# A decoder layer on one core: one product of v placed behind the third outer products, a later first turn in the drain, and small weights loaded ahead of the mixtures

## The chip, the core and the metric

The kernel runs on one core of one Trainium2 chip, in float32. The metric is the device time of one execution in microseconds (us). It is compared as the median of several executions; one further execution was taken by the profiler, and every row of a profile is from that one.

## The reference, cut to what matters

The layer has three parts, each added to x (32 sequences of 64 tokens, 512 wide, so 2048 tokens):

```python
x = x + attention(layernorm(x))       # 32 heads of 128; q and k get a bias and an rmsnorm with gains
x = x + cross_attention(layernorm(x), ctx)   # 64 x 64 weights Wq, Wk, Wv, Wskip
x = x + experts(layernorm(x))         # router 512 -> 64, top 8, mixture of expert biases
```

In the attention, `q = rmsnorm(xn @ Wq + bq) * gq`, the same for k, `v = xn @ Wv + bv`, and `out = softmax(q k^T / sqrt(128)) v @ Wo + bo`. The four projections (512 by 4096, and 4096 by 512) are nearly all of the arithmetic.

## The kernel before, in words

**Projections by Strassen's scheme.** A 2 by 2 block product is made with seven block products instead of eight. Tokens go in halves of the batch (two), a half in two quads of 512 tokens; heads go in 16 groups of two. For each half, the first head group takes its quads one by one (`single`, L1183). The other 15 take both quads together in a `Window` (L609, run by `double`, L1194): there q and k use the scheme twice over, an outer product that is itself made of seven inner ones. So there are 30 windows.

**A window's order of work is written by hand.** TensorE (PE in the profile), VectorE (DVE), ScalarE (ACT) and GpSimd (POOL) each run their instructions in program order. `Window.project` (L696) goes through four sets n = 0 to 3 of outer products: (1, 5), (2, 6), (7, 3) and (4). Each set is cut into four pieces m = 0 to 3 by the `yield`s of `outer` (L632). A piece issues p_w products on PE (L640) and DVE or ACT instructions that take their results out of PSUM (L651, L661, L664, L654). After each piece come, in this order: the entry of the table `behind` (L722), one waiting DVE step, and the entry of the table `plan` (L1201). I write (n, m) for such a place. The entries of `behind` that matter here are

```python
                (2, 2): lambda: (add(0, (1, 0), (1, 1)), add(0, (1, 1), (0, 1)), squares(1, 0, 0)),
                (2, 3): lambda: (add(1, (1, 0), (1, 1)), squares(1, 1, 0), squares(1, 0, 1)),
```

`add` with a first argument of 0 is a POOL addition, with 1 a DVE addition (both L719). `squares` is an ACT activation (L341) of the sum just made.

**v's products.** The plan also places v's seven products for each of the two quads (`values`, L363): one `v` in the plan is one product of 8 matmul instructions in the trace (L372). Their order is 1, 2, 6, 5, 7, 4, 3. Products 1, 6, 7 and 4 all add up in one PSUM tile, `va`, and after each of them ACT copies `va` to SBUF (L388), so that the next of them must wait for that copy. Products 2, 5 and 3 use the tile `vb`; DVE adds them to the copies (L392). In the kernel before, the first quad has its seven at (0,0) to (0,3) and (1,0) to (1,2), the second at (2,0) to (2,3) and (3,0) to (3,2).

**The rest of the attention** is pushed along by `Line` (L1137): `scale` multiplies q and k by their inverse norms (DVE L529, POOL L527, after a DMA of the norms), `attend` makes scores (L540), softmax (L254 to L262) and mixtures (L577), `turn` transposes the probabilities (L246).

**The drain.** After the last window, `drain` (L1321) makes the output projection of the first two token tiles (`plain_out`, 32 chunks of 8 matmul instructions, L822), and between chunks the line's remaining steps; `go(k)` runs k chunks. From chunk 24 on, DVE and POOL make the sums of Wo for Strassen's scheme (`wo_sums`, L858 to L866).

**The tails' start.** Then a new pool is opened. SyncE's queue (SP) issues nearly every DMA in program order, and so an issue that must wait holds up all that follow. In the kernel before it issues, in this order: bo_b; the mixtures a22, a11 and a21 of pair 1 (L806, 1 MB each); x for tile 3 (L173), whose buffer comes free when POOL has added bo to tile 1 (L810); eight small loads of the cross-attention's weights into `xw` (L214); rwt, rb_b and eb_sb. POOL fills `xw` with zeros first (L1372). PE makes five chunks of pair 1's output (product 2 of `strassen_out`, L869, on a mixture loaded earlier, is four of them; the fifth is the first of product 4, on a22), then two transposes of `xw` (L1392) and a product of them (L1396), and goes on with pair 1. Pairs 1 to 7 then run with the cross-attention and the experts of the tiles ahead (the tails) between their chunks.

Of the kernel before, what the change touches and what calls it, by code (L numbers as in the profile page):

```python
# [41 lines left out]
def decoder_layer(  # L42
# [37 lines left out]
    def block(name):  # L80
        return blocks.tile([P, BLK], F32, tag="blk", name=name)
# [130 lines left out]
    def load(to, what):  # L212

        tc.keep_in_program_order(nc.sync.dma_start(out=to, in_=what))  # L214
# [53 lines left out]
    def take_waiting():  # L268
        if waiting:
            waiting.pop(0)()  # L270
# [532 lines left out]
    def load_mixed(t, h, it):  # L803

        it = it.rearrange("p (g n) -> p g n", n=P)
        nc.sync.dma_start(out=it, in_=mixed[t // NQ][:, h, t % NQ, :, :])  # L806
        return it
# [41 lines left out]
    def wo_sums(b):  # L849

        four = four_blocks("wo_t")
        t1, t2 = (
            [it.rearrange("p (g f) -> p g f", f=DH) for it in two] for two in (four[0:2], four[2:4])
        )
        t4 = []
        for half in range(2):
            b11, b12, b21, b22 = (b[k][n][half] for k in range(2) for n in range(2))
            nc.vector.tensor_tensor(t1[half], b12, b11, ALU.subtract)  # L858
            nc.vector.tensor_tensor(t2[half], b22, t1[half], ALU.subtract)
            if half == 1:  # L860
                yield
            t4.append(block(f"wo_t4{half}").rearrange("p (g f) -> p g f", f=DH))
            nc.vector.tensor_tensor(t4[half], b21, t2[half], ALU.subtract)
        for half in range(2):
            b12, b22 = (b[k][1][half] for k in range(2))
            nc.gpsimd.tensor_tensor(b12, b22, b12, ALU.subtract)  # L866
        yield {1: b[0][0], 2: b[1][0], 3: b[1][1], 4: t4, 5: t1, 6: t2, 7: b[0][1]}
# [313 lines left out]
    line = Line()  # L1181
# [12 lines left out]
    def double(window, more):  # L1194

        v = window.v

        def end():
            line.attend(window.sums_of_squares, window.deviations)

        plan = [  # L1201
            [[v], [v], [v, line.scale], [v]],
            [[v, line.scale], [v, line.turn], [v], [line.attend, line.scale]],
            [[v, line.scale], [v], [v], [v]],
            [[v], [v], [v, line.turn], [*more.pop((3, -1), ()), end]],
        ]
        for (n, m), them in more.items():
            plan[n][m].extend(them)
        window.project(plan)
        line.add(*window.units)  # L1210
# [24 lines left out]
    for n, (hg, half) in enumerate(groups):  # L1235
# [29 lines left out]
        else:  # L1265
# [30 lines left out]
            if n + 1 == len(groups):  # L1296
                four = four_blocks("wo_0")
                wo_b = [[load_wo(k, 0, four[2 * k : 2 * k + 2])] for k in range(2)]
                a_0 = [[load_mixed(0, h, block(f"a0_{h}")) for h in range(HG)]]
            double(Window(units, w, half), more)  # L1300
    for k in range(2):
        wo_b[k].append(load_wo(k, 1, [block(f"wo{k}1{i}") for i in range(2)]))
# [18 lines left out]
    def drain():  # L1321
        fill = iter(todo)

        def go(count):
            for _ in range(count):
                next(fill)
                take_waiting()

        go(1)
        line.turn()  # L1330
        go(4)
        line.scale()
        go(4)
        line.scale()
        go(3)
        line.attend()
        line.scale()
        go(4)
        line.scale()
        go(1)  # L1340
        line.turn()
        go(2)
        line.attend()
        go(4)
        line.turn()
        go(1)
        line.attend()
        a12 = load_mixed(2, 1, block("a12_1"))
        sums = wo_sums(wo_b)
        next(sums)  # L1350
        for _ in fill:
            pass
        return a12, sums
# [4 lines left out]
    a_0.append([load_mixed(1, 0, block("a1_0")), load_mixed(1, 1, rest)])  # L1358
    todo = plain_out(0, a_0, wo_b, start_tail)
    a12, sums = drain()  # L1360
    assert not waiting and not coming
    ordered.close()
# [2 lines left out]
    bo_b = work.tile([P, D], F32, tag="bo", name="bo_b", bufs=1)  # L1365
    load(bo_b, bo.partition_broadcast(P))
    (right,) = sums
    outs = {1: strassen_out(1, right, start_tail, a12)}
    next(outs[1])

    xw = work.tile([P, 4, P], F32, tag="xw", name="xw", bufs=1)
    nc.gpsimd.memset(xw, 0.0)  # L1372
    for j, src in enumerate((xwq_t, xwk_t, xwv_t, xws_t)):
        for b in range(2):
            half = slice(b * SEQ, (b + 1) * SEQ)
            load(xw[half, j, half], src)
    rwt = work.tile([P, KC, NEXP], F32, tag="rwt", name="rwt", bufs=1)
    load(rwt, rw_t.rearrange("(kc p) e -> p kc e", p=P))
    rb_b = work.tile([P, NEXP], F32, tag="rb", name="rb_b", bufs=1)
# [4 lines left out]
    nc.gpsimd.memset(eb_sb[NEXP:P, :], 0.0)  # L1384
    nc.gpsimd.memset(wds, 0.0)
    load(eb_sb[0:NEXP, :], eb)
    for _ in range(4):
        next(outs[1])

    pt = ps_t.tile([P, 2, P], F32, tag="pt", name="pt_xw")  # L1390
# [64 lines left out]
```

## Time and profile before, and how to read it

| | |
|---|---|
| median of 3 executions | 1939.29 us (1936.71 to 1942.11) |
| the profiled execution | 1943.95 us |
| its span, first to last instruction | 1942.2 us, 1.75 us less |
| mean granted TensorE clock | 0.989 |
| PE busy | 1891.5 us, 97% of the span |
| DVE, POOL, ACT busy | 1211.4, 1046.5 and 643.6 us |
| one window, from one to the next at the same place | 42.34 us (603.60 to 645.93) |
| windows of the first half, of the second | from about 77 to 690 us, and from about 767 to 1391 us |
| drain | from 1393.4 us |
| tails' start | about 1464.5 us |

A row of a timeline gives the start in us from the span's beginning, the duration in us (of several merged instructions, from the first's start to the last's end), engine, source line, operation, output and inputs, the number of merged instructions, and in brackets the idle time of that engine before it with what ended it. PE's matmuls overlap a little: a row of four p_w instructions lasts 1.03 us, but the next row can start 0.86 us after it. Such distances from start to start are what a matmul costs when PE does not wait.

### The profile page before, as it was taken

To read this page: it belongs to the slowest core of one execution; us is meant where nothing else is said; L and a number is where in the kernel's file an instruction comes from. 1 tells how busy PE (TensorE), PEld (TensorE's weight loads), DVE (VectorE), ACT (ScalarE), POOL (GpSimd) and SP (SyncE) were. 2 spreads that over 40 slices of the span, in tenths; PEclk is the share of its full clock that TensorE was granted. 3 is DMA by queue.
4 is the path that set the end of the run, shared out by engine and by line. 5 is a ranking of instruction groups with operands and counts; after the bars stand their busy time and mean duration, and the time that the engine had idled before them with its cause. 6 is when DMAs were issued, how large, how long until landed. Compare 5 with 4: busy or idle time off the path is not lost.

```text
span 1942.2 us, 40532 instructions
## 1 busy us (share of the span) xinstructions
PE 1891.5 (97%) x16877; PEld 1628.0 (84%) x16877; DVE 1211.4 (62%) x2024; ACT 643.6 (33%) x1567; POOL 1046.5 (54%) x816
## 2 busy tenths in 40 slices
PE   8999999999999999999999999999998999999997
PEld 7888888888888878888888888888887888888875
DVE  5766767766667667766666666666545445554545
ACT  2244334344433443334433333443311112221122
POOL 4865667665567548666557666655225323332320
PEclk9999999999999999999999999999999999999998
DMA  4234333333433343333443333344933232223100
GB/s 132 66 99 129 123 111 109 110 99 117 131 125 100 109 141 101 101 107 99 127 133 113 110 109 100 99 130 135 300 118 128 90 106 70 69 90 112 49 20 22
DMA packets 162264, 210.72 MB, mean 108 GB/s; under 512 B 9888, under 2 KB 134880, under 8 KB 157984
## 3 DMA queue, kind: packets, MB, share of 16 engines
q1 hardware_dynamic: 160896, 207.05, 33.1%
q8 instruction: 133, 2.18, 0.5%
q10 hardware_dynamic: 1184, 1.08, 0.2%
q14 instruction: 51, 0.42, 0.1%
HBM read 169.82 MB, written 38.27 MB: 107 GB/s over the span
## 4 chain that ended last, share of the span: by engine, by line
PE 76%; DVE 11%; POOL 7%; issue 3%; DMA 2%; ACT 1%; SPq 0%; POOLq 0%; DVEq 0%; ACTq 0%
PE p_w L640 24%; PE py L822 18%; PE va L372 7%; PE vb L372 6%; POOL qk L719 5%; PE s L540 3%; PE ms_w L764 3%; PE o L577 3%; DVE qk L651 3%; DVE qk L664 3%; PE pa L430 1%; PE pt_p L246 1%; DVE qk L529 1%; DVE sums L259 1%; PE e_x L998 1%
## 5 line engine op out<-in xcount | busy, mean ns | idle before, releaser
L640 PE MATMUL p_w<-x,w 128*128 128x256 f32 x2940 | 726.0, 384 | 13.1 <-DVE qk L651 8.9
L640 PEld LDWEIGHTS p_w<-x,w 128*128 128x128 f32 x2940 | 522.3, 191 | 76.0 <-DVE qk L651 15.5
L651 DVE TENSOR_TENSOR qk<-p_w,qk 128x512 f32<-128x512 f32 x360 | 213.0, 599 | 148.6 <-PE p_w L640 113.0
L341 ACT ACTIVATE sq<-qk 128x512 f32<-128x512 f32 x256 | 158.2, 629 | 397.4 <-POOL qk L719 227.2
L372 PEld LDWEIGHTS va<-w,x 128*128 128x128 f32 x2048 | 265.3, 192 | 28.6 <-ACT v L388 18.3
L372 PE MATMUL va<-w,x 128*128 128x128 f32 x2048 | 277.2, 279 | 0.5 <-ACT v L388 0.5
L822 PE MATMUL py<-wo,a 128*128 128x256 f32 x1152 | 262.5, 381 | 0.0
L664 DVE TENSOR_TENSOR qk<-p_w,qk 128x512 f32<-128x512 f32 x360 | 219.7, 619 | 58.8 <-PE p_w L640 55.3
L120 POOL TENSOR_TENSOR w<-w 128x768 f32<-128x768 f32 x126 | 247.2, 1973 | 2.4
L822 PEld LDWEIGHTS py<-wo,a 128*128 128x128 f32 x1152 | 213.9, 190 | 35.6 <-issue 7.3
L262 POOL TENSOR_TENSOR prob<-prob,inv 128x512 f32<-128x512 f32 x64 | 76.7, 1198 | 293.5 <-DVE inv L261 292.5
L527 POOL TENSOR_TENSOR qk<-qk,rs 128x512 f32<-128x512 f32 x128 | 169.2, 1322 | 118.7 <-DMA rs<-row_w 98.6
L372 PEld LDWEIGHTS vb<-w,x 128*128 128x128 f32 x1536 | 202.3, 192 | 9.8
L372 PE MATMUL vb<-w,x 128*128 128x128 f32 x1536 | 203.3, 275 | 0.0
L388 ACT COPY v<-va 128x256 f32<-128x256 f32 x256 | 94.8, 370 | 320.5 <-PE va L372 320.4
L529 DVE SCALAR_TENSOR_TENSOR qk<-qk,gqk,rs 128x512 f32<-128x512 f32 x128 | 166.4, 1300 | 11.6 <-DMA rs<-row_w 10.2
L822 PE MATMUL py<-wo_t,a 128*128 128x256 f32 x608 | 142.2, 384 | 0.0
L822 PEld LDWEIGHTS py<-wo_t,a 128*128 128x128 f32 x608 | 114.6, 192 | 16.2 <-issue 0.8
L719 POOL TENSOR_TENSOR qk<-qk 128x512 f32<-128x512 f32 x60 | 90.3, 1504 | 60.6 <-DVE qk L664 58.2
L254 DVE TENSOR_REDUCE mx<-s 128x8 f32<-128x512 f32 x64 | 44.2, 691 | 110.0 <-PE s L540 110.0
L392 DVE TENSOR_TENSOR v<-vb,v 128x256 f32<-128x256 f32 x192 | 80.7, 420 | 47.9 <-PE vb L372 27.3
L592 ACT ACTIVATE ot<-o,bvt 128x256 f32<-128x256 f32 x256 | 99.2, 469 | 2.2 <-PE o L577 2.2
(177 smaller groups left out, 2191.4 us busy)
## 6 DMA issues: line engine op xcount, KB each, us to landing
rs<-row_w SPq DMA_DIRECT2D x120, 512.0 KB
mixed<-ot SPq DMA_DIRECT2D x64, 512.0 KB
a<-mixed SPq DMA_DIRECT2D x32, 1024.0 KB
w<-in_wq_dram SPq DMA_DIRECT2D x64, 256.0 KB
w<-in_wk_dram SPq DMA_DIRECT2D x62, 256.0 KB
w<-in_wv_dram SPq DMA_DIRECT2D x62, 256.0 KB
wo<-in_wo_dram SPq DMA_DIRECT2D x8, 1024.0 KB
x<-in_x_dram SPq DMA_DIRECT2D x28, 256.0 KB
```

Of the source, the lines that this page charges most:

```text
L120: on.tensor_tensor(*(it.rearrange("p c j d -> p (c j) d") for it in (out, a, b)), ALU.subtract)
L341: nc.scalar.activation(sq, of, AF.Square)
L372: nc.tensor.matmul(to[:, j, :], left[i][:, c, j, :], right[i][:, c, 2, :], start=first and j == 0 and c == 0, stop=c == 1, skip_group_chec ...
L388: nc.scalar.copy(self.v[h, ab], what)
L527: nc.gpsimd.tensor_tensor(k, k, rk, ALU.mult)
L529: lambda: nc.vector.scalar_tensor_tensor(q, q, gqk, rq, ALU.mult, ALU.mult)
L592: nc.scalar.activation(ot[:, h, :, b * SEQ : (b + 1) * SEQ], o[b][:, h, :, :], AF.Identity, bias=bvt[:, hg * HG + h : hg * HG + h + 1],)
L640: nc.tensor.matmul(bank[:, s, :], self.w.inner[o][i], inner_x[self.half, o][i], start=first and s == 0, stop=True, skip_group_check=True,)
L651: nc.vector.tensor_tensor(to(t, j), bank, add(t, j), ALU.add)
L664: nc.vector.tensor_tensor(to(t, j), bank, to(t, j), ALU.add)
L719: on.tensor_tensor(qk[to], qk[to], qk[what], ALU.add)
L822: nc.tensor.matmul(py, a[:, g, :], b[g // KH][:, g % KH, :], start=n == 0 and g == 0, stop=n == last and g == NHG - 1,)
```

## The change

Three edits. One `v` goes from place (0, 3) to place (2, 3), where there are now two, so that the first quad's last product of v (product 3) comes at (2, 0), and the second quad's seven at (2, 1), (2, 2), twice at (2, 3), and at (3, 0) to (3, 2). In the drain the first turn comes after three chunks rather than one, and the two scales behind it after six and nine chunks rather than five and nine. At the tails' start, the zeros and the eight loads of `xw` stand ahead of pair 1's mixtures in the program, and pair 1 gets six chunks rather than five ahead of the transposes of `xw`.

```diff
@@ double, L1201 @@
         plan = [
-            [[v], [v], [v, line.scale], [v]],
+            [[v], [v], [v, line.scale], []],
             [[v, line.scale], [v, line.turn], [v], [line.attend, line.scale]],
-            [[v, line.scale], [v], [v], [v]],
+            [[v, line.scale], [v], [v], [v, v]],
             [[v], [v], [v, line.turn], [*more.pop((3, -1), ()), end]],
         ]
@@ drain, L1329 @@
-        go(1)
+        go(3)
         line.turn()
-        go(4)
+        go(3)
         line.scale()
-        go(4)
+        go(3)
         line.scale()
@@ tails' start, L1365 @@
     (right,) = sums
-    outs = {1: strassen_out(1, right, start_tail, a12)}
-    next(outs[1])
 
     xw = work.tile([P, 4, P], F32, tag="xw", name="xw", bufs=1)
     nc.gpsimd.memset(xw, 0.0)
@@
             load(xw[half, j, half], src)
+    outs = {1: strassen_out(1, right, start_tail, a12)}
+    next(outs[1])
     rwt = work.tile([P, KC, NEXP], F32, tag="rwt", name="rwt", bufs=1)
@@
-    for _ in range(4):
+    for _ in range(5):
         next(outs[1])
```

## The prediction, made before the changed kernel had run

> **What bounds the kernel now.** First the page's busy times: PE is at work for 97% of the span, so only two things move the end, PE's work and PE's waits. The change adds no matmul and drops none.
>
> ```profile
> PE 1891.5 (97%) x16877; PEld 1628.0 (84%) x16877; DVE 1211.4 (62%) x2024; ACT 643.6 (33%) x1567; POOL 1046.5 (54%) x816
> ```
>
> Then the list of waits, for who keeps whom (total us, times, longest). ACT's squares (L341) wait for POOL's additions (L719) twice in each of the 30 windows, up to 9.5 us. ACT has time for that; the second line shows where it reaches PE, in the weight loads of v's products behind ACT's copies, 58 times, about two per window.
>
> ```profile
> ACT sq L341 <- POOL qk L719: 227.2, 60, 9.5
> PEld va L372 <- ACT v L388: 18.3, 58, 0.9
> ```
>
> Then the timeline of one window's end, all engines. It starts at place (2, 2).
>
> ```profile
> 640.93 1.05 PE L372 MATMUL va<-w,x 128*128 128x128 f32 x8
> 640.96 1.27 DVE L664 TENSOR_TENSOR qk<-p_w,qk 128x512 f32<-128x512 f32 x2
> ...
> 642.31 3.11 POOL L719 TENSOR_TENSOR qk<-qk 128x512 f32<-128x512 f32 x2 [2.16 <-DVE qk L664]
> 642.68 1.05 PE L372 MATMUL vb<-w,x 128*128 128x128 f32 x8
> ...
> 643.62 0.63 ACT L341 ACTIVATE sq<-qk 128x512 f32<-128x512 f32 x1 [6.47 <-POOL qk L719]
> 644.16 0.35 ACT L388 COPY v<-va 128x256 f32<-128x256 f32 x1
> 644.56 1.16 PE L372 MATMUL va<-w,x 128*128 128x128 f32 x8
> ...
> 645.45 1.15 ACT L341 ACTIVATE sq<-qk 128x512 f32<-128x512 f32 x2 [0.94 <-POOL qk L719]
> 645.46 0.42 DVE L651 TENSOR_TENSOR qk<-p_w,qk 128x256 f32<-128x256 f32 x1 [1.16 <-POOL qk L719]
> 645.93 1.13 PE L640 MATMUL p_w<-x,w 128*128 128x256 f32 x4 [0.21 <-DVE qk L651]
> ...
> 646.51 0.35 ACT L388 COPY v<-va 128x256 f32<-128x256 f32 x1
> 646.91 1.16 PE L372 MATMUL va<-w,x 128*128 128x128 f32 x8
> ```
>
> To be seen: DVE ends (2, 2) at 642.23, POOL makes two additions until 645.42, and three things hang on the second: a DVE step at 645.46 that holds PE (0.21 us), and ACT's two squares. PE's product of v at 646.91 starts 0.05 us after ACT's copy ended at 646.86. Last, the same view at the tails' start:
>
> ```profile
> 1463.03 0.53 POOL L1372 MEMSET xw<- 128x512 f32 x1
> ...
> 1464.52 1.89 PE L822 MATMUL py<-wo_t,a 128*128 128x256 f32 x8
> ...
> 1467.56 1.20 SPq L214 DMA_DIRECT2D xw<-in_xwq_t_dram  x2
> ...
> 1470.42 0.45 PE L1392 MATMUL pt_xw<-ident,xw 128*128 128x128 f32 x1 [4.01 <-POOL x L810]
> ```
>
> PE waits 4.01 us for loads issued behind the x of tile 3.
>
> **What the Trainium skill says.** "Perfetto Trace Analysis", section "Tensor Engine Instruction (MATMUL, LD_WEIGHTS)": ACT, DVE and GpSimd are strict FIFO. The trace agrees: PE had ended v's product 6 at 641.98, but its copy ran at 644.16, behind a square queued ahead of it. "GPSIMD Engine Reference", section "1. Specifications": its SBUF interfaces are shared with VectorE, with contention when a DVE instruction has two SBUF inputs. The trace agrees: L529, with two such inputs, took 0.70 us at 637.33 and 2.35 at 620.59, beside two of POOL's L120. "TensorE: Matmul & The Clock Gate", section "What's actually happening": an idle window of about 3.4 us halves the clock, a busy one restores it. The trace agrees: PE idle from 1466.41, granted clock 0.50 from about 1470 until 1476.8, and 24 matmuls from 1473.01 took 7.04 us, where they take 5.19 at full clock: 1.85 us lost.
>
> **Edit 1, v's product: what it removes.** The v product moved is 5, eight matmuls without a copy of its own; its addition on DVE goes with product 7's. At (2, 3) PE gets 0.89 us more work (eight v matmuls, start to start). The wait before (3, 1) goes: the v row ahead takes 1.37 us rather than 0.89 (644.56 to 645.93), the p_w row before it 0.99 rather than 0.86, in all 0.61 us per window. At (0, 3) PE reaches (1, 0) 0.89 us sooner. The bank that its second product needs was freed by a DVE step that ended at 620.67, before PE gets there at 622.4, so nothing waits at once.
>
> **Edit 1: what is late next.** v's products shift by one place, so the second quad's product 6 now stands at (2, 3), not at (2, 2). Its copy therefore stands on ACT behind the entries of `behind` at both (2, 2) and (2, 3): three squares, two of which wait for POOL's additions. The order of the built programs confirms it: before square, copy, square, square, copy; now square, square, square, copy, copy. And product 7, at (3, 0), adds into `va` and must wait for that copy. Before, the copy in this place was product 7's, and product 4 waited for it at 646.91. Now product 7 starts there at the earliest, and behind it lie what PE had done by then: one v product and one piece, 0.89 + 0.87 (four p_w, 0.86 to 0.87) = 1.76 us. Product 4 then needs product 7's copy, 0.17 us of drain and 0.37 of copy, covered by the piece at (3, 1). So PE is 1.76 us later at (3, 2), if the second addition ends when it did. That 1.76 already contains the removed wait, since it is counted against the recorded place.
>
> **Edit 1: does the addition move?** Two shifts, neither shown in the trace before. (a) PE's lead from (0, 3): at most 0.89 us. It is cut at the scores (L540, 631.68), which need POOL's L527, ended 631.06: not over 0.56 us is kept. If DVE's L529, now 0.9 us sooner, falls badly between two POOL instructions, none is kept. I take 0.3; ends 0.56 and 0. (b) On DVE one addition for v (0.41 us) comes ahead of the (2, 2) steps, product 3's, and one (product 2's) goes behind them: zero, with 0.25 either way for what L529 meets on the shared interface. Per window 1.76 - 0.3 = 1.45 us later; ends 0.95 and 2.0. Thirty windows: +43.5, ends 28.5 and 60.
>
> **Edit 2, the drain.** PE waits 1.33 us for POOL's probabilities before the first turn (at 1396.68). Two more chunks, 3.46 us, cover it: -1.4 with the refill (0.1). The scales come at chunk 6 and 9 for 5 and 9; both wait for the norms' DMA until 1402.6, and the scores at chunk 12 had 3 us and more to spare. What hides this turn is PE's own chunks.
>
> **Edit 3, the tails' start.** The order of the built program leaves the zeros of `xw` behind POOL's two L866, so they still end at 1463.56. The first `xw` load waits for them, and the three mixtures, issued from 1446.7 on before, now stand behind it on SP. Eight issues at 0.63 us (1467.56 to 1472.58) end at 1468.6; then a22. Its time to land: two mixtures issued from 1475.43 were through by about 1482.4, so I take 4.3 us for the first, 3.4 to 5.9 as bounds: 1473. PE needs it at 1464.5, for product 4's first chunk; xw's transposes no longer wait for theirs. The x of tile 3, issued at about 1470 for 1467.2, is first used at 1480, so product 4 hides it; rwt, rb_b, eb_sb and ctx come no later than before. From 1473: two chunks 3.46, half clock 1.85, transposes and their product 1.2, two chunks 3.46: 1483.0, against 1480.1. Later PE waited 1.70 us at 1492.72 for a copy behind slow DVE steps; with PE later, that wait shrinks by 0 to 1.7. I take +2 (0 to +4.5). If a22 had come in time, the edit would have gained some 5.
>
> **The sum.** 43.5 - 1.4 + 2 = +44.1. The profiled execution, 1943.95 (span 1942.2 plus 1.75), becomes 1988.0. It lies 4.66 above the median of the runs shown; on the median 1939.29 that is 1983.4.
>
> **The rivals.**
> 1. The forecast, 0.62: the copy behind three squares. With the ends above 1939.3 + 28.5 - 1.4 + 0 = 1966 to 1939.3 + 60 - 1.4 + 4.5 = 2002.
> 2. Faster, 0.11: product 7 finds its copy ready. Then the 0.61 us per window goes and nothing replaces it: -18.3 - 1.4 + 2 = -17.7, 1921.6. It decides at one point: PE reaches product 7 at about 645.3 in the window shown, the copy ends at 646.86, so POOL's second addition would have to end 1.5 us sooner. For it: DVE's (2, 2) steps could come up to 0.4 us sooner, and PE's lead adds 0.5. Against: that is 0.9 of 1.5.
> 3. Smaller, 0.15: both shifts beyond my ends, PE's 0.89 kept whole and 0.45 on DVE, leaving 0.4 per window: +12 + 0.6, 1952. Against: scores waiting for L527.
> 4. Larger, 0.12: PE loses 0.3 at (1, 3) as well, since product 7's addition on DVE (0.41 us) now stands between L529 and the step that PE waits for there, which ended only 0.2 us before PE came (630.49 against 630.72): 2.3 per window, +69 + 0.6, 2009.
>
> **How the numbers follow.** The predicted time is case 1, 1983.4. A measurement of this kernel tells about 0.3% (6 us) from no change. Case 2 is all of faster, 0.11; a sixth or so of case 3 and of the border to case 2 is within 0.3%, 0.05; slower 0.84. Range 1950 to 2008: case 1, nearly all of 3, half of 4; case 2 and half of 4 are left out.
>
> **What would show it.** Right: in windows, PE idle of over 1 us before a `va` product of L372, released by ACT's L388; that copy after three L341; the list of waits with some 40 us of PE under ACT v L388; no wait of L640 for DVE L651 at (3, 1); a window of about 43.8 us for 42.34; the wait before the first drain transpose gone; PE idle from about 1464 to 1473, ended by a DMA of a mixture. Wrong: windows of 41.7 us, or the copy before 645.5 in the window's own time, or a22 landing by 1465.

## The result and the profile after

The changed kernel takes 1984.71 us (median of 5, 1978.0 to 1986.28); the kernel before, beside it, 1939.49 (median of 5, 1936.71 to 1942.85). The ratio is 1.022, with a 95% interval of 1.0204 to 1.0236. The profiled execution took 1985.12 us, its span 1983.2, 41.0 more than before. PE does the same work in it (1890.5 us busy, 1891.5 before); what was added is waiting:

```profile
PE 1890.5 (95%) x16877; PEld 1632.9 (82%) x16877; DVE 1243.0 (63%) x2024; ACT 645.5 (33%) x1567; POOL 1048.2 (53%) x816
```

The list of waits of the changed kernel (total us, times, longest) names four waits of PE that the kernel before lacks or has smaller:

```profile
PE va L372 <- ACT v L388: 30.0, 29, 3.5
...
PE p_w L640 <- DVE qk L651: 12.4, 25, 1.2
...
PE py L822 <- DMA a<-mixed: 9.6, 1, 9.6
...
PE pm_f L1086 <- DVE inv_x L1024: 8.0, 1, 8.0
```

The first PE line was expected (0.5 us before), and so was the one for the DMA of a mixture. Before, the p_w line was 8.9 us and stood mostly ahead of (3, 1); it is now at another place. The last line is new. In the kernel before, two rows at (2, 0) matter, of which the prediction names the first:

```profile
637.33 0.70 DVE L529 SCALAR_TENSOR_TENSOR qk<-qk,gqk,rs 128x512 f32<-128x512 f32 x1
637.58 1.35 POOL L262 TENSOR_TENSOR prob<-prob,inv 128x512 f32<-128x512 f32 x1 [1.34 <-DVE inv L261]
```

The timeline of a window's end in the changed kernel shows the first two waits (the same places as before, from (2, 0) on):

```profile
654.26 0.37 DVE L392 TENSOR_TENSOR v<-vb,v 128x256 f32<-128x256 f32 x1
654.55 1.63 DVE L529 SCALAR_TENSOR_TENSOR qk<-qk,gqk,rs 128x512 f32<-128x512 f32 x1
654.59 1.04 POOL L262 TENSOR_TENSOR prob<-prob,inv 128x512 f32<-128x512 f32 x1
...
656.84 1.99 PE L640 MATMUL p_w<-x,w 128*128 128x256 f32 x8 [0.54 <-DVE qk L651]
...
659.64 2.62 POOL L719 TENSOR_TENSOR qk<-qk 128x512 f32<-128x512 f32 x2 [2.33 <-DVE qk L664]
...
662.29 1.23 ACT L341 ACTIVATE sq<-qk 128x512 f32<-128x512 f32 x2 [0.72 <-POOL qk L719]
...
663.43 0.35 ACT L388 COPY v<-va 128x256 f32<-128x256 f32 x1
...
663.84 1.16 PE L372 MATMUL va<-w,x 128*128 128x128 f32 x8 [0.60 <-ACT v L388]
```

At the bottom is the forecast wait: product 7 of v stands behind a copy that stands behind two squares that waited for POOL. At the top is one that was not forecast: DVE adds a product of v first, then its L529 takes 1.63 us beside POOL's L262, and PE waits 0.54 us at (2, 2) for the DVE step behind it.

Which of L529 and L262 waits is not the same in every window. In 17 of the 28 windows it is L529, as here; PE then waits about 0.47 us at (2, 2) and 0.60 us for the copy, and 16 of these windows take 43.10 to 43.24 us. In the other 11, L529 starts 0.05 us or more ahead of L262, and L262 is the one that waits:

```profile
524.52 0.74 DVE L529 SCALAR_TENSOR_TENSOR qk<-qk,gqk,rs 128x512 f32<-128x512 f32 x1
524.57 1.59 POOL L262 TENSOR_TENSOR prob<-prob,inv 128x512 f32<-128x512 f32 x1
...
533.83 1.16 PE L372 MATMUL va<-w,x 128*128 128x128 f32 x8 [1.43 <-ACT v L388]
```

There PE waits less at (2, 2), in most of them not at all (0.76 us in one), but POOL's two additions end later in the window (in all but the first of the 11) and PE waits 1.42 us or more for the copy: these windows take 43.21 to 44.28 us.

Two rows further up in the window that starts at 626 us matter for the account of the prediction, the third L527 of a window and the scores at (1, 3):

```profile
648.21 1.27 POOL L527 TENSOR_TENSOR qk<-qk,rs 128x512 f32<-128x512 f32 x1
648.62 1.15 PE L540 MATMUL s<-qk 128*64 128x64 f32 x32
```

At the tails' start the loads of `xw` come right after the zeros, and the three mixtures behind them; PE had run out of work at 1494.75:

```profile
1493.09 0.52 POOL L1370 MEMSET xw<- 128x512 f32 x1
...
1493.64 1.45 SPq L214 DMA_DIRECT2D xw<-in_xwq_t_dram  x2
...
1498.97 1.53 SPq L806 DMA_DIRECT2D a<-mixed  x3
...
1504.34 5.44 PE L822 MATMUL py<-wo_t,a 128*128 128x256 f32 x16 [9.59 <-DMA a<-mixed]
```

And 85 us later, in the second pair of tiles:

```profile
1578.40 4.50 POOL L946 TENSOR_TENSOR a<-a,a 128x2048 f32<-128x2048 f32 x1 [14.07 <-PE py L822]
...
1587.43 1.26 POOL L810 TENSOR_TENSOR x<-x,bo_b 128x512 f32<-128x512 f32 x1
1588.72 0.42 DVE L942 TENSOR_TENSOR x<-x,py 128x256 f32<-128x256 f32 x1 [5.73 <-POOL x L810]
...
1589.29 2.05 PE L1086 MATMUL pm_f<-eb_sb,wt_f 128*128 128x512 f32 x2 [7.96 <-DVE inv_x L1024]
```

POOL's L810 (bo added to x) stands behind two additions of 4.5 us of pair 2, DVE's L942 waits for it, and everything queued behind L942 on DVE waits too, the step that PE needs among it. In the kernel before, POOL ran that L810 ahead of L946 (1545.64) and L947 (1550.35), and PE did not wait:

```profile
1544.08 1.26 POOL L810 TENSOR_TENSOR x<-x,bo_b 128x512 f32<-128x512 f32 x1 [12.61 <-DMA x<-in_x_dram]
```

Stage by stage, from PE's rows of the two traces:

| stretch | before | after | difference |
|---|---|---|---|
| to the drain's first chunk | 1393.36 | 1424.97 | +31.6 |
| from there until PE is ready for product 4 | 71.2 | 69.6 | -1.5 |
| product 4, with the transposes of `xw` | 15.5 | 19.6 | +4.1 |
| wait for `kvs` | 1.70 | 0.26 | -1.4 |
| stall in pair 2 | 0 | 7.96 | +8.0 |

They sum to +40.8 of the span's +41.0. The first row is the least certain, since it compares one execution with one: the four runs below that leave the program unchanged up to the drain reach its first chunk at 1387.8 to 1389.4 us, 4 to 6 us ahead of this execution of the kernel before. Their windows take the same time; the difference lies ahead of the windows and between the two halves. This is probably also where most of the gap lies between the 41.0 us of the spans and the 45.2 us of the medians.

### The profile page after: what moved, and what is told of

It is laid out like the page before. It is cut to its first block, busy times and chain, and to the rows that moved or that the text cites. A ratio compares the mean times of both kernels' runs of the same rounds, so it can differ in the third digit from the quotient of the medians.

```text
span 1983.2 us, 40532 instructions
## 1 busy us (share of the span) xinstructions
PE 1890.5 (95%) x16877; PEld 1632.9 (82%) x16877; DVE 1243.0 (63%) x2024; ACT 645.5 (33%) x1567; POOL 1048.2 (53%) x816
## 4 chain that ended last, share of the span: by engine, by line
PE 75%; DVE 10%; POOL 7%; issue 3%; DMA 2%; ACT 2%; SPq 0%; POOLq 0%; DVEq 0%; ACTq 0%
PE p_w L640 25%; PE py L822 18%; PE va L372 9%; PE vb L372 4%; POOL qk L719 4%; PE o L577 3%; PE s L540 3%; PE ms_w L764 3%; DVE qk L529 2%; DVE qk L651 2%; DVE qk L664 2%; PE pa L430 1%; ACT sq L341 1%; PE pt_p L246 1%; DVE sums L259 1%
## 5 line engine op out<-in xcount | busy, mean ns | idle before, releaser
L372 PEld LDWEIGHTS va<-w,x 128*128 128x128 f32 x2048 | 269.7, 194 | 53.6 <-ACT v L388 41.7
L388 ACT COPY v<-va 128x256 f32<-128x256 f32 x256 | 95.5, 373 | 495.8 <-PE va L372 495.8
L341 ACT ACTIVATE sq<-qk 128x512 f32<-128x512 f32 x256 | 159.6, 630 | 250.4 <-POOL qk L719 157.2
L262 POOL TENSOR_TENSOR prob<-prob,inv 128x512 f32<-128x512 f32 x64 | 73.2, 1145 | 314.5 <-DVE inv L261 313.5
L527 POOL TENSOR_TENSOR qk<-qk,rs 128x512 f32<-128x512 f32 x128 | 173.0, 1351 | 124.9 <-DMA rs<-row_w 89.2
L529 DVE SCALAR_TENSOR_TENSOR qk<-qk,gqk,rs 128x512 f32<-128x512 f32 x128 | 171.9, 1343 | 11.5 <-DMA rs<-row_w 9.9
L719 POOL TENSOR_TENSOR qk<-qk 128x512 f32<-128x512 f32 x60 | 81.4, 1356 | 60.2 <-DVE qk L664 57.9
L392 DVE TENSOR_TENSOR v<-vb,v 128x256 f32<-128x256 f32 x192 | 79.3, 413 | 53.6 <-PE vb L372 27.4
```

What stands on the lines that cost most here:

```text
L341: nc.scalar.activation(sq, of, AF.Square)
L372: nc.tensor.matmul(to[:, j, :], left[i][:, c, j, :], right[i][:, c, 2, :], start=first and j == 0 and c == 0, stop=c == 1, skip_group_chec ...
L388: nc.scalar.copy(self.v[h, ab], what)
L527: nc.gpsimd.tensor_tensor(k, k, rk, ALU.mult)
L529: lambda: nc.vector.scalar_tensor_tensor(q, q, gqk, rq, ALU.mult, ALU.mult)
L719: on.tensor_tensor(qk[to], qk[to], qk[what], ALU.add)
```

## Experiments

All are kernels of the same program with a few lines changed, timed beside the kernel before. "Window" is the median distance of 28 windows on PE (from one row of L764 to the next) in the profiled execution.

| run | window, us | median, us | ratio to before (95%) |
|---|---|---|---|
| kernel before | 42.34 | 1939.5 to 1940.4 | |
| changed kernel | 43.12 | 1984.71 | 1.022 (1.0204 to 1.0236) |
| plan_alone | 43.10 | 1971.25 | 1.0155 (1.0133 to 1.0176) |
| squares_after_v6 | 42.64 | 1945.02 | 1.0023 (1.0013 to 1.0032) |
| squares_after_v7 | 42.63 | 1945.92 | 1.0027 (1.0015 to 1.004) |
| before_squares_late | 42.26 | 1938.97 | 0.9991 (0.9984 to 0.9997) |
| scale_ahead_alone | 42.47 | 1957.67 | 1.0097 (1.0081 to 1.0113) |
| scale_ahead_of_v | 41.51 | 1922.63 | 0.991 (0.9896 to 0.9925) |
| drain_alone | as before | 1939.77 | 0.9996 (0.9988 to 1.0003) |
| tails_alone | as before | 1955.3 | 1.0067 (1.0052 to 1.0081) |
| load_order_alone | as before | 1942.72 | 1.0015 (1.0008 to 1.0022) |
| six_chunks_alone | as before | 1947.71 | 1.0037 (1.0026 to 1.0048) |
| zeros_early | 42.34 | 1932.07 | 0.9964 (0.9952 to 0.9976) |
| all_mended | 41.51 | 1910.77 | 0.9848 (0.9835 to 0.986) |

**The windows: is it the copy's place?** First the plan's two lines alone.

> Edit 1 alone: the plan's v moved, drain and tails' start as before. Between the windows' first and last marks the changed kernel lost 31.6 us. If that is the plan's doing and nothing else's, this kernel is 31 to 32 us over the kernel before, 1970 to 1972, the drain's wait of 1.33 us before its first transpose and the tails' start are as before, and there is no stall of 8 us near the second pair of tiles. If the windows are slowed by something the other edits bring along (another placement of buffers), it is well under that, 1940 to 1960. If the plan is also behind the late stall in the tails, it is near 1980.

The ratio gives +30 us (1.55% of 1940), so the windows' 31.6 us are the plan's own; the late stall is not there. Then the copy of product 6 was put ahead of the two squares of (2, 3), and in the next run product 7's copy too:

```diff
-                (2, 3): lambda: (
-                    add(1, (1, 0), (1, 1)),
-                    squares(1, 1, 0),
-                    squares(1, 0, 1),
-                ),
+                (2, 3): lambda: add(1, (1, 0), (1, 1)),
...
                     for it in plan[n][m]:
                         it()
+                    if (n, m) == (2, 3):    # squares_after_v7: (3, 0)
+                        squares(1, 1, 0)
+                        squares(1, 0, 1)
```

> Edit 1 alone, with the two squares of (2, 3) issued on ACT behind the plan's v's of (2, 3), not ahead of them, so that the copy of product 6 stands behind one square and not behind three; PE's order is that of edit 1 alone. Theory A (the copy's place in ACT's queue): the wait for ACT's copy ahead of product 7 is gone, the copy ends some 1.4 us sooner, and a window takes 41.9 to 42.6 us for 42.34 before: 1928 to 1948. Theory B (the windows are longer because PE has 0.89 us more at (2, 3), or because DVE's additions of v now fall beside POOL's instructions, and the copy is only where the wait shows): another wait takes its place, a window stays above 43 us, and the time is 1962 to 1972.

> As the one before, with the two squares behind product 7's copy too, at (3, 0). Theory A: no copy of v stands behind a square that waits for POOL's second addition; both waits for ACT's copies in a window's end go, those of the kernel before (18.3 us in 58) among them, and a window takes 41.7 to 42.3 us: 1921 to 1938. If PE then meets the DVE step that waits for the second addition ahead of (3, 1), some 0.2 to 0.6 us per window come back, up to 1945. Theory B: over 43 us a window, 1962 to 1972.

The wait for the copy ahead of product 7 is gone in both, and with it 26 of the 31 us (by the medians): theory A's mechanism holds. Its size for the second run does not: 1945.92, just beyond even the 1945 that it allowed for, and a window of 42.63 us where 41.7 to 42.3 was expected (42.64 for the first run, at the edge of its range). Both windows still hold the 0.47 us at (2, 2), and some 0.3 us ahead of the piece at (3, 2), behind DVE's L719, which now takes 1.5 us beside POOL. So theory B has a share: DVE's additions of v do fall beside POOL's instructions. The same move of the squares in the kernel before:

> The kernel before with its plan, and only the two squares of (2, 3) issued behind product 7's copy at (3, 0). Tells what of the run before this is the squares' place alone. Theory A: the waits for copies at a window's end go (about half of 18.3 us), the wait of 0.21 us for the DVE step ahead of (3, 1) stays: 4 to 10 us faster, 1929 to 1935. If the wait for the copy was covered by that for the addition's other readers, no change: 1937 to 1941.

0.09% faster (0.03 to 0.16%): the second outcome. PE no longer waits for the copy ahead of product 4, but the wait for the addition's other reader, 0.23 us at (3, 1), is untouched.

**The remainder: DVE's order at (2, 0).** In the kernel before, the v at (2, 0) is a product without an addition on DVE. In the changed kernel it is the first quad's product 3, and `v` issues its addition (L392) and only then takes the waiting step, L529. One word in the plan turns that round:

```diff
-            [[v, line.scale], [v], [v], [v, v]],
+            [[take_waiting, v, line.scale], [v], [v], [v, v]],
```

It was tried on top of squares_after_v7, and on edit 1 as it was made:

> Edit 1 with the two squares behind product 7's copy, and at (2, 0) the waiting DVE step (the scaling L529, 0.70 us undisturbed) taken ahead of the plan's v, so that DVE runs it ahead of the addition of product 3 (L392, 0.4 us), not behind it. With the squares out of the way a window still took 42.6 us for 42.34 before, with one wait left, 0.47 us at (2, 2) for a DVE step (L651), behind an L529 of 1.56 us that started beside POOL's L262. Theory: the addition's place on DVE is that remainder. L529 takes 0.7 to 0.8 us again, the wait at (2, 2) goes, and a window takes 42.0 to 42.2 us: 1929 to 1936. If L529 is as long as before ahead of the addition, the wait stays at 0.4 to 0.5 us and the time at 1944 to 1947.

> Edit 1 as made, squares where they were, and only the waiting DVE step (L529) taken ahead of the plan's v at (2, 0). If the two costs add (theory A: the copy's place is worth 25 us of the 31, the DVE addition's place the other 6, and 18 below that once both are mended), the wait ahead of product 7 for ACT's copy is still here and only the wait at (2, 2) is gone: 1955 to 1966. If the wait for the copy is itself mostly lateness of DVE's steps handed on by POOL's additions (theory D), most of it goes too: 1925 to 1942.

The timeline of scale_ahead_of_v at (2, 0) to (3, 0):

```profile
628.15 0.70 DVE L529 SCALAR_TENSOR_TENSOR qk<-qk,gqk,rs 128x512 f32<-128x512 f32 x1
628.40 1.35 POOL L262 TENSOR_TENSOR prob<-prob,inv 128x512 f32<-128x512 f32 x1 [0.60 <-DVE inv L261]
628.77 0.42 DVE L392 TENSOR_TENSOR v<-vb,v 128x256 f32<-128x256 f32 x1
...
630.02 1.89 PE L640 MATMUL p_w<-x,w 128*128 128x256 f32 x8
...
636.16 1.05 PE L372 MATMUL va<-w,x 128*128 128x128 f32 x8
```

L529 is ahead of POOL's L262 by 0.25 us and takes 0.70 us; neither PE row waits. The time is 1922.63, 0.9% under the kernel before; it lies below the range expected, since the wait at (3, 2) went as well. With the squares where they were, the same word brings 1957.67: the wait for the copy stays (0.68 us), so it is not lateness of DVE handed on, and theory D falls. Both causes are real, and mended together they give 48.6 us, more than the 25.3 and 13.6 that each gives alone (by the medians). In a median window this shows as a wait that stays: with only the squares moved, 0.73 us at (2, 2) and 0.39 around (3, 2) are left; with only L529 moved, 0.96 around the copy.

**The drain.**

> Edit 2 alone: the drain's first turn after three chunks. The wait of 1.33 us before it goes, with 0.1 for the refill, and nothing takes its place: -1.4 us, 1938 to 1939.5; its profile shows no wait before the first transpose of the drain. If another wait takes its place, 1939.3 to 1941.

By the clock this is undecided (0.12% faster to 0.03% slower holds both outcomes). In its trace the wait before the first transpose is gone, nothing new waits, and from the drain's first chunk to product 4 it takes 69.6 us for 71.2.

**The tails' start.** The whole edit, and its two halves: the order of loads with `range(4)`, and `range(5)` with the loads as before.

> Edit 3 alone: small weights ahead of the mixtures, and six chunks. The trace of the changed kernel gives it some 4 us up to the end of product 4, less 1.4 for a copy's wait that shrinks, and 8 us in a stall of 7.96 us ahead of a product with eb_sb in the second pair of tiles, which the kernel before does not have: +10.6, 1949 to 1953. If the stall is a matter of phase between this edit and the windows, it is +2 to +4, 1941 to 1944.

> Edit 3's order of loads, with five chunks as before. If the stall of 7.96 us comes from the sixth chunk (theory S, by way of POOL's order: the two additions of 4.5 us of the second pair, L946 and L947, then stand ahead of the x of its first tile, L810), there is no stall here and only the late mixture counts: +2.5 to +4, 1942 to 1944.5. If it comes from the late loads (theory L, SP's order), the stall is here: +9 to +11, 1948 to 1951.

> Edit 3's sixth chunk alone, with the loads in the order of before. Theory S: POOL has L946 and L947 of the second pair ahead of L810, the stall of about 8 us is here, and the wait of 4.0 us for xw's loads shrinks by the chunk's 1.7: +5 to +7, 1944 to 1947. Theory L: no stall, -1.7 to 0, 1937 to 1940.

tails_alone is a little above the range expected (+13.0 by its ratio), and so is six_chunks_alone. The halves tell the two causes apart, though their ratios sum to 10.1 and not 13.0, which the intervals allow. The load order alone costs 2.9 us and has PE's wait for the mixture (9.2 us), but no stall. The sixth chunk alone costs 7.2 us and has the stall:

```profile
1538.34 4.51 POOL L946 TENSOR_TENSOR a<-a,a 128x2048 f32<-128x2048 f32 x1 [14.07 <-PE py L822]
...
1547.37 1.26 POOL L810 TENSOR_TENSOR x<-x,bo_b 128x512 f32<-128x512 f32 x1
...
1549.24 2.04 PE L1086 MATMUL pm_f<-eb_sb,wt_f 128*128 128x512 f32 x2 [7.97 <-DVE inv_x L1024]
```

That is theory S. After the drain (from `ordered.close()`), the order on DVE, ACT and POOL is no longer written by hand; the planner sets it when the program is built. One chunk more ahead of the loop over pairs shifts pair 2's chunks against the tails, and the planner then puts L946 and L947 ahead of L810. POOL's rows in the traces show it: L810, L946, L947 in the kernel before and in load_order_alone; L946, L947, L810 in the changed kernel, tails_alone and six_chunks_alone. How the planner comes to this order is not shown.

Then the mixture. `xw` got a buffer of its own at the program's start, with its zeros written there, the loads ordered as in the change and five chunks:

```diff
     ones = const.tile([P, 32], F32, tag="ones", name="ones")
+    xw = const.tile([P, 4, P], F32, tag="xw", name="xw")
     nc.gpsimd.memset(ones, 1.0)
...
     nc.gpsimd.memset(ln_eps, LN_EPS)
+    nc.gpsimd.memset(xw, 0.0)
...
-    xw = work.tile([P, 4, P], F32, tag="xw", name="xw", bufs=1)
-    nc.gpsimd.memset(xw, 0.0)
     for j, src in enumerate((xwq_t, xwk_t, xwv_t, xws_t)):
```

> The order of loads of edit 3 with five chunks, but with xw in a buffer of its own, filled with zeros by POOL near the program's start. Theory: the mixture a22 was late only since the loads of xw ahead of it on SP waited for zeros that stood behind two POOL instructions of Wo's sums. Then SP issues xw's loads and the mixtures from about 1447 on, a22 is there before 1460, PE waits neither for a mixture (9.2 us in the run with the order alone) nor for xw (4.0 us before), the clock is not halved: 4 to 6.5 us faster than before, 1933 to 1936. If the mixtures wait for something else there (a buffer, PE), the wait for a22 stays and it is 1941 to 1944.

```profile
1442.80 2.31 SPq L216 DMA_DIRECT2D xw<-in_xwq_t_dram  x2
...
1449.17 5.53 SPq L808 DMA_DIRECT2D a<-mixed  x3
...
1460.61 1.89 PE L824 MATMUL py<-wo_t,a 128*128 128x256 f32 x8
1462.34 0.38 PE L1392 MATMUL pt_xw<-ident,xw 128*128 128x128 f32 x2
```

PE waits neither for a mixture nor for `xw`, and the kernel is 7 us faster than before by the ratio (0.9964), with a median just under the range expected. So the order of loads was a sound idea held up by where the zeros stood.

**All of it together**: scale_ahead_of_v, the drain's edit and zeros_early.

> The three edits with what the runs so far mend: squares behind product 7's copy, L529 ahead of the addition at (2, 0), the drain's turn after three chunks, xw's loads ahead of the mixtures with their zeros written near the start, five chunks. If the gains add: -17.7 - 1 - 8 = -27, 1911 to 1916. If they cover each other in part, 1916 to 1922.

1910.77 us, 1.5% faster than the kernel before and just under the range for gains that add. Its windows are 41.51 us and PE has no wait of 8 us in its tails.

## Why the prediction was right, and where its sum was not

The direction and the main mechanism were right. That the total is so close (1983.4 for 1984.71) is luck: two errors cancel. By the stages the windows were put 12 us too dear and the tails 9 us too cheap; by the ratios of plan_alone and tails_alone it is 13 and 11. The 0.76 us per median window lies under the 0.95 that the prediction gave as its lower end; the mean, 0.98 in the changed kernel, is just inside.

- **"Product 7 starts there at the earliest": right in kind.** PE waits for a copy behind three squares, 30.0 us in 29 windows. In a window of plan_alone it costs PE 0.86 us: 0.76 before product 7, and 0.10 in the row after a wait.
- **"Does the addition move?": the term that was mis-sized.** The prediction let 0.3 of 1.76 us come off, at most 0.8 with both ends. Counted from the window's start (PE's row of L764), POOL's second addition ended at 37.12 us before and at 36.06 in plan_alone, 1.06 sooner. PE's lead was not cut at the scores, it was kept whole (0.89), because the prediction took the wrong instruction to hold them. The L527 that ended at 631.06 is the third of the window and belongs to the scaling at (1, 3), which the plan puts behind the scores. In the two rows of the changed kernel shown above, the scores start 0.86 us before that L527 ends. Of the 0.89, 0.63 was lost at (2, 2); POOL's first addition started 2.80 us after (2, 2) for 3.11; and the two additions took 2.62 us for 3.11. 0.89 - 0.63 + 0.31 + 0.49 = 1.06. So product 7 started 0.98 us ahead of product 4's old place, and 1.76 - 0.98 = 0.78 is left, against 0.76 measured between the two medians of a window. With some windows longer the mean is +0.98 in the changed kernel, 27.5 us over 28; the rest of the 31.6 lies outside these 28.
- **"(b) ... zero, with 0.25 either way": wrong.** The addition that moved ahead of the (2, 2) steps moved ahead of an L529 too, and that put L529 behind POOL's L262: 1.56 us for 0.70 in plan_alone, and 0.73 us of PE in a median window (0.63 ahead of the piece at (2, 2) and 0.10 in it). "SBUF — State Buffer" of the Trainium skill, section "SBUF: two separate sides", says that of a DVE instruction with two SBUF inputs and a GpSimd instruction that reads SBUF, the one that starts second is blocked until the first ends. The traces agree in the main: in plan_alone L262 ran from 648.99 to 650.03, L529 started at 649.02, and 1.01 of waiting and 0.70 of work would make 1.71 (1.56 measured); with L529 first by 0.25 us, POOL's L262 took 1.35 us for 1.04. They differ where the two start within 0.05 us of each other: the L529 shown above at 654.55 starts 0.04 us ahead of L262 and is still the one that waits. The prediction named the L529 at 637.33, and one that falls badly between two POOL instructions as the case in which the lead is lost. It gave that no weight, and did not ask which of L529 and L262 would now come first.
- **"In all 0.61 us per window" removed: too little.** With no wait left a window is 41.51 us, so the kernel before lost 0.83: 0.61 in the two rows ahead of (3, 1), and 0.22 in the next two, the piece at (3, 1) and product 4 (0.98 and 1.00 us for 0.87 and 0.89). So edit 1 gave back 0.83 and lost 0.73 + 0.86, and 42.34 - 0.83 + 1.59 = 43.10.
- **Rival 2 (faster)** named the condition rightly: the copy ready when PE comes, and a time of 1921.6 with all edits. scale_ahead_of_v meets it and takes 1922.63 with edit 1 alone, by other means than an earlier addition: it also moves the squares and L529.
- **The signs named**: PE's idle time before product 7 is 0.60 us in a median window where over 1 was expected, PE's line under ACT v L388 30.0 for some 40, and a window 43.10 for 43.8. The others came: three L341 ahead of the copy, no wait at (3, 1), no wait at the drain's first transpose, and a wait of 9.6 us for a mixture.
- **Edit 2**: -1.4 forecast, -1.5 in the trace.
- **Edit 3, the late mixture: right.** +2 forecast with 0 to +4.5 around it; +2.7 by the stages (4.1 - 1.4), +2.9 by load_order_alone's ratio. The mixture landed 5.4 us after its issue for the 4.3 taken.
- **Edit 3, the sixth chunk: missed.** The sum gave it no cost of its own. It cost 8.0 us, 85 us past the place of the edit. POOL's order, which tells it, was read for the zeros and not for the pairs behind.

What stays open: what brings L529 ahead of L262 in 11 windows of the changed kernel and in 5 of plan_alone, and some longer windows besides (one of 44.07 has a wait of 0.70 us earlier, at (1, 1)). The median of a window does not carry the whole time either. In scale_ahead_alone it is 0.13 us over the kernel before, 4 us in 30 windows, and the mean is 0.30 over, 9 us; the time is 18 us longer. The remainder was not traced to a wait.

## What to carry to other kernels

When a step is moved, follow what it issues on every engine: a product moved on PE carried a copy on ACT behind three squares, and an addition on DVE ahead of a step that ran a race with POOL, and each alone cost about as much (0.86 and 0.73 us) as all the waits that the move removed (0.83). Where the first of two engines' instructions makes the other wait, an addition of 0.4 us ahead of one of them became a loss of 0.7 us per window, so ask of each such pair who will now start first. And where a planner sets the order, compare the built order of all engines well past the edit, not only at it.

## What the runs showed of the hardware that was not expected

- Which of DVE and POOL waits is decided by less than 0.1 us. L529 starting 0.25 us before L262 took 0.70 us. Starting 0.06 or 0.07 us before it, L529 took 0.74 and L262 1.57 or 1.58. Starting up to 0.04 us after it, L529 took 1.55 to 1.59. With a lead of 0.04 or 0.05 us it went either way in the changed kernel and plan_alone.
- Slower DVE instructions can be good: DVE's L719 took 1.46 us for 0.69 in plan_alone. It started during POOL's second addition (0.36 us after its start), where before it had started 0.06 us ahead of it. The two additions then took 2.62 us for 3.11, and they were the ones that ACT and PE waited for.
- After a wait, PE's next row of p_w loses a further 0.10 us: eight matmuls step 1.83 us for 1.73.
